# A transformer chain on one core: constants made early, the first layer's last closing on VectorE, weight loads moved

## The chip, the cores and the metric

The kernel runs on one core of one Trainium2 chip. The metric is the device time of that core in microseconds (us). The median of three runs of the kernel before is 1660.57 us (1658.11 to 1660.71). The work is in float32 throughout, so every matrix product on TensorE is issued as two passes, and counts in the trace are twice those in the code.

## The reference

Four layers follow one another on an activation `x` of 64 sequences of 64 tokens, each a row of 128 numbers; the same shape of context, `ctx`, goes beside it.

```python
x = L0(x, ctx)   # relative-position attention, 16 heads of 64 over ctx+x; LN, relu MLP, LN
x = L1(x, ctx)   # self attention and cross attention (16 heads of 8, masks), relu MLP; three LN
x = L2(x, ctx)   # a gate from pooled ctx, LN
x = L3(x, ctx)   # self and cross attention, then 8 experts, the best two of each token
# the end of L0:
out = layer_norm(x + ctx_heads @ Wo, ln1_g, ln1_b) * non_pad_mask
out = layer_norm(out + relu(out @ W1 + b1) @ W2 + b2, ln2_g, ln2_b) * non_pad_mask
```

A layer norm is `(x - mean) / sqrt(var + eps) * g + b` over the 128 numbers of a token.

## The kernel before

**Tiling.** The 4096 tokens are cut into 8 groups of 512. A group is a tile of 128 partitions by 512: four blocks of 128 tokens side by side.

**First layer** (`first_layer`, L381). One software pipeline, `for t in range(-REL, n)` (L627), runs over 64 steps: 8 groups times 8 pairs of heads. A step t issues parts of several pairs: the transposed weights and products of pair t, the scores of t+2, keys of t+3, the position scores of t+5. The emitted order is kept on every engine in this layer. Small jobs are hung onto single steps: `pads()` at 0, `later(t)` at 0 to 7, `block_diagonal()` from 12. After a group's eighth pair its closing generator `close` (L574) is started, and it is advanced once a step beside the next group: transpose, layer norm, affine, MLP, layer norm, affine. The last closing, of group 7, is not advanced there; it is handed on in `ends`, together with what is left of group 6.

**The norm.** `normalise` (L289) takes mean and variance on VectorE, then the inverse root: with `quick` false one power on GpSimd, with `quick` true eleven small operations on VectorE (`inverse_root`, L276). With a mask (`npm`) GpSimd multiplies the factor by it, and VectorE applies mean and factor in four operations. `affine` (L325) then multiplies by `g` and adds `b` times the mask, three operations on GpSimd; the product of `b` and mask is in a tile `oT`, of which there are two.

**Second part** (`other_layers`, L987). `drive` (L152) runs the generators of the remaining phases in rounds: self attention, cross attention and so on for each group, new ones admitted every few rounds, and the leftover closings `ends` in front of them. A further generator, `fill` (the experts), is stepped once a round. Here the framework's scheduler orders each engine's instructions by priorities; the order is fixed when the kernel is built, and each engine works strictly in it. PSUM tiles come from 7 rotating buffers (`pmm`, L120) and one further buffer, `extra` (L123), which holds the attention products `av` and some small results. All DMAs of the SyncE and ScalarE queues share eight completion semaphores in turn, so a new one waits for the eighth last one.

**Between the two parts.** The memory of the first layer is given up and taken anew, so the first instructions of the second part wait for the last of the first. In the kernel before these stand there:

- on ScalarE's queue, the loads of `w2l`, `in3`, `wo3` and `rw` (L992 to L995), and later the sixteen expert weight loads of `load_expert` (L1548), called in `layer2` (L1297);
- on GpSimd, the constants of the router and the experts (`desc`, `tri`, `ones`, `tok`, `base0`, `start`, `limit`, `index`, `lane`: memsets, `iota`s, one select), then memsets of two tiles `vb`;
- on VectorE, the copies of those `iota`s into float32;
- on TensorE, four transposes of the experts' biases into `extra` (`pfb`, L1520), which VectorE copies into `fc1bT` (L1523).

Of the kernel before, what the change touches and what calls it, by code (L numbers as in the profile page):

```python
# [9 lines left out]
I32 = mybir.dt.int32  # L10
# [3 lines left out]
ALU = mybir.AluOpType  # L14
AX = mybir.AxisListType

P = 128
B = 64
S = 64
D = 128  # L20
NB = 8
T = NB * S
NBLK = T // P
# [74 lines left out]
def kernel(ctx: ExitStack, tc: tile.TileContext, a: dict, out: bass.AP):  # L98
# [16 lines left out]
    def wtile(shape, tag, bufs, dtype=F32):  # L115
        if tag in COMMON:
            return pools["common"].tile(shape, dtype, tag=tag, bufs=COMMON[tag], name=tag)
        return pools["work"].tile(shape, dtype, tag=tag, bufs=bufs, name=tag)
# [22 lines left out]
    def v3(ap, n):  # L141
        return ap.rearrange("p (a b) -> p a b", a=n)
# [5 lines left out]
    def mid(ap, n):  # L148

        return ap.unsqueeze(1).to_broadcast([ap.shape[0], n, ap.shape[1]])  # L150
# [65 lines left out]
    yrows = dram.tile([2 * B * S, D], F32, tag="yrows", name="yrows", bufs=1)  # L216
    PADS = 5

    def block_diagonal():

        nc.vector.tensor_reduce(
            hm, ident.rearrange("p (h e) -> p h e", e=8), axis=AX.X, op=ALU.add
        )
        nc.vector.tensor_reduce(
            m4, hm.rearrange("p (g j) -> p j g", j=4), axis=AX.X, op=ALU.add
        )

        for i in range(2):  # L230
            yield
            blocks = wtile([P, 3, P], "T", 4)
            for k in range(3):
                nc.vector.tensor_tensor(
                    blocks[:, k, :].rearrange("p (h e) -> p h e", e=8),
                    mid(bd_small[:, 3 * i + k, :], 16),
                    last(hm[:, :], 8),
                    ALU.mult,
                )
            yield  # L240
            pt = pmm("bdt")
            for k in range(3):
                nc.tensor.transpose(pt[:, k * P : (k + 1) * P], blocks[:, k, :], ident)
            turned = wtile([P, 3, P], "T", 4)
            nc.vector.tensor_copy(turned, v3(pt[:, 0 : 3 * P], 3))
            yield
            pf = pmm("fold")
            nc.tensor.matmul(pf[:, 0:P], lhsT=turned[:, 2, :], rhs=turned[:, 1, :], start=True, stop=True)
            nc.tensor.matmul(pf[:, P : 2 * P], lhsT=turned[:, 0, :], rhs=wo1[:, i, :], start=True, stop=True)
            yield  # L250
            nc.vector.tensor_copy(qk1[:, i, :], pf[:, 0:P])
            nc.vector.tensor_copy(wo1[:, i, :], pf[:, P : 2 * P])
# [36 lines left out]
    def normalise(dst, src, npm=None, width=D, quick=False):  # L289

        st = wtile([P, NBLK, 6], "st6", 4)
        mv = wtile([P, NBLK, 2], "mv", 4)
        rs = wtile([P, NBLK], "rs", 4)
        for k in range(NBLK):
            nc.vector.bn_stats(st[:, k, :], src[:, k * P : (k + 1) * P])
        for k in range(NBLK):
            nc.vector.bn_aggr(mv[:, k, :], st[:, k, :])
        nc.vector.tensor_scalar(
            rs, mv[:, :, 1:2].rearrange("p a b -> p (a b)"), EPS, None, ALU.add
        )  # L300
        if quick:
            inverse_root(rs)
        else:
            nc.gpsimd.tensor_tensor(rs, rs, nhalf, ALU.pow)
        if npm is not None:
            nc.gpsimd.tensor_tensor(rs, rs, npm, ALU.mult)
        yield
        if npm is None:
            nm = wtile([P, NBLK], "nmr", 4)
            nc.vector.scalar_tensor_tensor(  # L310
                nm, mv[:, :, 0:1].rearrange("p a b -> p (a b)"), -1.0, rs, op0=ALU.mult, op1=ALU.mult
            )
        for k in range(NBLK):
            ks = slice(k * P, (k + 1) * P)
            if npm is None:
                nc.scalar.activation(
                    dst[:, k * width : k * width + D], src[:, ks], AF.Identity,
                    scale=rs[:, k : k + 1], bias=nm[:, k : k + 1],
                )
            else:  # L320
                nc.vector.tensor_scalar(
                    dst[:, ks], src[:, ks], mv[:, k, 0:1], rs[:, k : k + 1], ALU.subtract, ALU.mult
                )

    def affine(dst, src, g, b, npm=None):  # L325
        nc.gpsimd.tensor_tensor(v3(dst[:, :], NBLK), v3(src[:, :], NBLK), mid(row(g), NBLK), ALU.mult)
        if npm is None:
            nc.gpsimd.tensor_tensor(v3(dst[:, :], NBLK), v3(dst[:, :], NBLK), mid(row(b), NBLK), ALU.add)
        else:
            bn = wtile([P, T], "oT", 2)  # L330
            nc.gpsimd.tensor_tensor(
                v3(bn[:, :], NBLK), mid(row(b), NBLK), last(npm, D), ALU.mult
            )
            nc.gpsimd.tensor_tensor(dst, dst, bn, ALU.add)

    LANDED = mybir.DependencyInfo(mybir.DependencyClass.Sync, mybir.DependencyReason.DATA)

# [43 lines left out]
    def first_layer():  # L381
# [191 lines left out]

        def close(g, zT):  # L574
            npm = cols[:, _C["npm"][0] + NBLK * g : _C["npm"][0] + NBLK * (g + 1)]
            o1 = turned(zT, "z", 4)
            yield
            yield from normalise(o1, o1, npm)
            affine(o1, o1, "l0_g1", "l0_be1", npm)
            yield  # L580
            o1T = turned(o1)
            add_row(o1, "l0_b2")
            yield
            hs = []
            hidden(o1T, w1_0, "l0_b1", hs, range(2))
            yield
            hidden(o1T, w1_0, "l0_b1", hs, range(2, 4))
            yield
            pf = tokens_by(lambda c: hs[c], lambda c: w2_0[:, c, :], NFC)
            yield  # L590
            z = wtile([P, T], "z", 2)
            nc.vector.tensor_tensor(z, pf, o1, ALU.add)
            yield from normalise(z, z, npm)
            affine(xs[g], z, "l0_g2", "l0_be2", npm)

        pad = wtile([P, PADS, ROWW], "pad", 1)

# [29 lines left out]
        for t in range(-REL, n):  # L627
# [40 lines left out]
                pads()  # L668
            if 0 <= t < 8:
                later(t)  # L670
            if t == 12:
                folds = block_diagonal()
            if t >= 12:
# [313 lines left out]
    def other_layers(ends):  # L987
# [1 line left out]
        in3 = wtile([P, 2, 3 * D], "in3", 1)  # L989
        wo3 = wtile([P, 2, D], "wo3", 1)  # L990
        rw = wtile([P, NE], "rw", 1)
        nc.scalar.dma_start(w2l, a["w2l"])  # L992
        nc.scalar.dma_start(in3, a["in3"])
        nc.scalar.dma_start(wo3, a["wo3"])
        nc.scalar.dma_start(rw, a["rw"])  # L995

        bkm = wtile([P, 2, 4], "bkm", 1)
        for i, name in enumerate(("sa_in_b", "ca_in_b")):
            nc.vector.tensor_scalar(bkm[:, i, :], m4, col(name, 1), None, ALU.mult)

        desc = wtile([P, NE], "desc", 1)
        for e in range(NE):
            nc.gpsimd.memset(desc[:, e : e + 1], float(NE - e))
        tri = wtile([P, P], "tri", 1)
        make_upper_triangular(nc, tri[:, :], diag=False)
        ones = wtile([P, P], "ones", 1)
        nc.gpsimd.memset(ones, 1.0)

        toki = wtile([P, NG * NBLK], "toki", 1, I32)
        nc.gpsimd.iota(toki, pattern=[[P, NG * NBLK]], base=0, channel_multiplier=1)  # L1010
        tok = wtile([P, NG * NBLK], "tok", 1)
        nc.vector.tensor_copy(tok, toki)

        base0 = wtile([P, NE], "base0", 1)
        bases = {0: base0}
        basei = wtile([P, NE], "basei", 1, I32)
        nc.gpsimd.iota(basei, pattern=[[REGION * P, NE]], base=0, channel_multiplier=0)
        nc.vector.tensor_copy(base0, basei)


        vbs = [wtile([P, NB, 8, 18], f"vb{i}", 1) for i in range(2)]
# [404 lines left out]
        def router(g, hT, x, zx):  # L1426
# [67 lines left out]
            for n in range(2):  # L1494
# [6 lines left out]
                for k in range(NBLK):  # L1501
# [13 lines left out]
                            )  # L1515
                    done["scatters"][h].append(sc.ins)
            done["routed"] += 1

        fb = cols[:, _C["fc1_b"][0] : _C["fc1_b"][1]].rearrange("p (e c) -> p c e", c=NFC)
        pfb = extra("pfb")  # L1520
        for c in range(NFC):
            nc.tensor.transpose(pfb[0:NE, c * P : (c + 1) * P], fb[:, c, :], ident)
        nc.vector.tensor_copy(fc1bT, v3(pfb[0:NE, :], NFC))  # L1523

        drive(
            [(self1, "attention"), (cross1, "attention"), (forward1, "light"), (layer2, "light"),
             (self3, "attention"), (cross3, "attention")],
            {"attention": 4, "light": 2},
            ends,
            experts(),  # L1530
        )

    done = {"scatters": [[] for _ in range(NH)], "routed": 0, "exponentials": False}
# [13 lines left out]

    def load_expert(e):  # L1548
        es = slice(e * D, (e + 1) * D)
        nc.scalar.dma_start(fcw[:, 0:NFC, es], a["fc1"][e].rearrange("p (c k) -> p c k", k=P))  # L1550
        nc.scalar.dma_start(fcw[:, NFC:, es], a["fc2"][e].rearrange("(f c) d -> c f d", c=P))

    start = mtile([P, NE], "start")
    limit = mtile([P, REGION], "limit")
    index = mtile([P, max(NSLOT)], "index")
    lane = mtile([P, 1], "lane")
    for dst, step, n, mult in (
        (start, REGION * P, NE, 0), (limit, P, REGION, 0), (index, 1, max(NSLOT), 0), (lane, 0, 1, 1)
    ):
        it = mtile([P, n], f"iota{n}", I32)  # L1560
        nc.gpsimd.iota(it, pattern=[[step, n]], base=0, channel_multiplier=mult)
        nc.vector.tensor_copy(dst, it)
    endbase = [mtile([P, NE], f"endbase{h}") for h in range(NH)]
    fc1bT = mtile([NE, NFC, P], "fc1bT")
    with stage("att", psx=1):
# [73 lines left out]
```

## Time and profile before

| | |
|---|---|
| median of three runs | 1660.57 us |
| the profiled execution's own time | 1656.37 us |
| its span, first to last instruction | 1654.6 us |
| busy in the span: VectorE, ScalarE, GpSimd | 1166.5, 992.8, 888.3 us |
| mean granted TensorE clock | 0.951 |
| first layer, 0 to 713 us: TensorE busy | 695.11 us, clock 1.00 |
| passage, 713 to 790 us: TensorE busy | 61.77 of 77 us, clock 0.82 |

The table's first three rows are three things: runs without a profiler, the one execution that the trace shows, and the stretch of it between first and last instruction. In the listings a row has its start, its duration, the engine, the operation, what it writes and reads, how many instructions are merged, and in brackets how long the engine was idle before and what released it. A row merged from several instructions starts with the first and covers the whole of them. "PEld" is the loading of a weight tile into TensorE, "ACTq" and "SPq" the issuing of DMAs by ScalarE's and SyncE's sequencers. All instructions carry line 77, since a helper records them, so rows are told apart by their tiles. In tables by stretch each engine has its busy us and, in brackets, its instructions; then come the granted clock (1.00 is full), the share of the DMA engines and GB/s.

### The profile page before, as it was taken

To read this page: it belongs to the slowest core of one execution; us is meant where nothing else is said; L and a number is where in the kernel's file an instruction comes from. 1 tells how busy PE (TensorE), PEld (TensorE's weight loads), DVE (VectorE), ACT (ScalarE), POOL (GpSimd) and SP (SyncE) were. 2 spreads that over 40 slices of the span, in tenths; PEclk is the share of its full clock that TensorE was granted. 3 is DMA by queue.
4 is the path that set the end of the run, shared out by engine and by line. 5 is a ranking of instruction groups with operands and counts; after the bars stand their busy time and mean duration, and the time that the engine had idled before them with its cause. 6 is when DMAs were issued, how large, how long until landed. Compare 5 with 4: busy or idle time off the path is not lost.

```text
span 1654.6 us, 45059 instructions
## 1 busy us (share of the span) xinstructions
PE 1524.2 (92%) x17469; PEld 1132.4 (68%) x17469; DVE 1166.5 (70%) x3226; ACT 992.8 (60%) x2711; POOL 888.3 (54%) x852
## 2 busy tenths in 40 slices
PE   6999999999999999978888999989989899868995
PEld 4666666666666666646666676666767667668995
DVE  4767686867677677758897688676776688756555
ACT  4666455555655565535776565656777777427774
POOL 2546373645555564666887576644332223367543
PEclk9999999999999999979999899898999899759998
DMA  6776544545455554241001000000000000113244
GB/s 171 157 172 160 141 138 127 136 132 144 121 144 132 144 135 107 56 140 34 12 15 31 24 24 20 9 8 8 2 2 15 21 2 7 35 54 86 74 116 125
DMA packets 215540, 131.40 MB, mean 79 GB/s; under 512 B 38416, under 2 KB 201490, under 8 KB 215328
## 3 DMA queue, kind: packets, MB, share of 16 engines
q1 hardware_dynamic: 186016, 90.52, 22.9%
q10 hardware_dynamic: 24992, 29.54, 5.7%
q0 software_dynamic: 4320, 8.47, 1.5%
q8 instruction: 139, 2.28, 0.6%
q14 instruction: 73, 0.60, 0.1%
HBM read 66.48 MB, written 62.47 MB: 78 GB/s over the span
## 4 chain that ended last, share of the span: by engine, by line
PE 65%; DVE 18%; ACT 6%; POOL 6%; DMA 3%; issue 2%; SPq 0%; ACTq 0%; DVEq 0%; POOLq 0%
PE av L77 8%; PE psv L77 8%; PE proj L77 7%; PE psk L77 6%; PE f L77 6%; PE pt L77 6%; PE tok L77 5%; DVE mx L77 4%; PE pbd L77 4%; DVE s L77 4%; PE psc L77 4%; PE acc L77 3%; PE tr L77 2%; ACT z L77 2%; PE sc L77 2%
## 5 line engine op out<-in xcount | busy, mean ns | idle before, releaser
L77 ACT ACTIVATE s<-s,nm 128x128 f32<-128x128 f32 x512 | 198.1, 388 | 236.8 <-DVE nm L77 220.5
L77 POOL TENSOR_TENSOR s<-s,sm 128x512 f32<-128x512 f32 x128 | 130.4, 1040 | 208.7 <-DVE sm L77 208.7
L77 PE MATMUL pt<-ident,s 128*128 128x128 f32 x1536 | 213.0, 282 | 19.3 <-DVE s L77 12.1
L77 POOL TENSOR_TENSOR s<-s,mx 128x512 f32<-128x512 f32 x160 | 164.4, 1046 | 99.8 <-DVE mx L77 93.6
L77 PEld LDWEIGHTS pt<-ident,s 128*128 128x128 f32 x1536 | 177.0, 145 | 41.2 <-issue 17.7
L77 POOL TENSOR_TENSOR skew<-skew,mb 128x512 f32<-128x512 f32 x128 | 159.9, 1270 | 70.7 <-DMA skew<-scr 70.2
L77 ACT ACTIVATE pT<-pt 128x512 f32<-128x512 f32 x256 | 140.5, 600 | 79.6 <-PE pt L77 71.3
L77 POOL TENSOR_TENSOR rs<-rs,nhalf 128x4 f32<-128x4 f32 x72 | 73.3, 1018 | 151.9 <-DVE rs L77 144.1
L77 PEld LDWEIGHTS av<-vb,pT 128*64 128x64 f32 x4096 | 132.2, 143 | 23.4 <-issue 12.4
L77 PE MATMUL av<-vb,pT 128*64 128x18 f32 x4096 | 140.4, 215 | 6.8 <-DVE o L77 4.8
L77 DVE TENSOR_REDUCE mx<-s 128x8 f32<-128x512 f32 x160 | 102.8, 675 | 40.1 <-ACT s L77 40.1
L77 PE MATMUL psv<-wv,kv 128*128 128x256 f32 x512 | 127.4, 392 | 0.0
L77 PE MATMUL psk<-kv,wk 128*128 128x512 f32 x256 | 127.0, 618 | 0.0
L77 PE MATMUL sc<-km,qs 32*64 32x256 f32 x2048 | 106.3, 422 | 8.9 <-ACT qs L77 4.4
L77 DVE COPY pT<-pt 128x512 f32<-128x512 f32 x128 | 82.0, 681 | 36.9 <-PE pt L77 36.9
L77 PEld LDWEIGHTS psv<-wv,kv 128*128 128x128 f32 x512 | 92.2, 189 | 15.1 <-issue 1.0
L77 PEld LDWEIGHTS pbd<-rT,qp 64*128 64x128 f32 x1024 | 62.1, 187 | 58.3 <-DVE qp L77 56.5
L77 PEld LDWEIGHTS av<-pT,v 128*64 128x64 f32 x2048 | 66.8, 138 | 50.9 <-issue 31.3
L77 DVE TENSOR_TENSOR s<-sc,mb 128x512 f32<-128x512 f32 x128 | 82.4, 680 | 25.0 <-PE sc L77 25.0
L77 POOL DMA_INDIRECT yrows<-km,tob x71 | 71.2, 1004 | 53.1 <-DVE tob L77 26.4
L77 DVE TENSOR_TENSOR s<-psc,skew 128x512 f32<-128x512 f32 x128 | 87.4, 683 | 13.9 <-issue 6.3
L77 ACT ACTIVATION_READ_ACCUMULATOR s<-s,nm 128x1 f32 x512 | 95.6, 187 | 0.0
(256 smaller groups left out, 3523.3 us busy)
## 6 DMA issues: line engine op xcount, KB each, us to landing
scr<-stage SPq DMA_DIRECT2D x64, 516.0 KB, 4.8
skew<-scr SPq DMA_DIRECT2D x128, 256.0 KB, 4.3
hrows<-pad ACTq DMA_DIRECT2D x53, 325.0 KB, 2.5
ctx<-in_ctxT SPq DMA_DIRECT2D x24, 256.0 KB, 2.6
km<-hrows SPq DMA_DIRECT2D x71, 65.0 KB, 2.0
fcw<-in_fc ACTq DMA_DIRECT2D x16, 256.0 KB, 4.0
kv<-in_xT SPq DMA_DIRECT2D x8, 256.0 KB, 4.9
kv<-in_ctxT SPq DMA_DIRECT2D x8, 256.0 KB, 5.4
```

The costliest lines, as they stand in the source:

```text
L77: ins = it(*args, **kw)
```

## The change

1. The router's and experts' constants are made in step 11 of the first layer by a function `constants()`, in tiles that live through the kernel.
2. `normalise` and `affine` of the last closing (`g == NG - 1`) run on VectorE: inverse root, multiplication by the mask, `g` and `b`. The two products of `b` and mask stay on GpSimd, issued at the closing's start.
3. A generator `prepared` goes before the experts': after four rounds it issues the loads of `in3`, `wo3`, `rw` and `w2l` on ScalarE's queue, after four more the transposes and the copy to `fc1bT`.
4. The sixteen expert weight loads go to SyncE's queue.

```diff
+    def constants():
+        for e in range(NE):
+            nc.gpsimd.memset(desc[:, e : e + 1], float(NE - e))
+        make_upper_triangular(nc, tri[:, :], diag=False)
+        nc.gpsimd.memset(ones, 1.0)
+        nc.gpsimd.iota(toki, pattern=[[P, NG * NBLK]], base=0, channel_multiplier=1)
+        nc.vector.tensor_copy(tok, toki)
...
+            nc.gpsimd.iota(it, pattern=[[step, n]], base=0, channel_multiplier=mult)
+            nc.vector.tensor_copy(dst, it)
...
-            nc.gpsimd.tensor_tensor(rs, rs, npm, ALU.mult)
+            (nc.vector if quick else nc.gpsimd).tensor_tensor(rs, rs, npm, ALU.mult)
...
+    def shift_of(b, npm):
+        bn = wtile([P, T], "oT", 2)
+        nc.gpsimd.tensor_tensor(v3(bn[:, :], NBLK), mid(row(b), NBLK), last(npm, D), ALU.mult)
+        return bn
+
-    def affine(dst, src, g, b, npm=None):
+    def affine(dst, src, g, b, npm=None, shift=None):
+        if shift is not None:
+            nc.vector.tensor_tensor(v3(dst[:, :], NBLK), v3(src[:, :], NBLK), mid(row(g), NBLK), ALU.mult)
+            nc.vector.tensor_tensor(dst, dst, shift, ALU.add)
+            return
...
+            quick = g == NG - 1
+            shift = [shift_of(b, npm) if quick else None for b in ("l0_be1", "l0_be2")]
             o1 = turned(zT, "z", 4)
             yield
-            yield from normalise(o1, o1, npm)
-            affine(o1, o1, "l0_g1", "l0_be1", npm)
+            yield from normalise(o1, o1, npm, quick=quick)
+            affine(o1, o1, "l0_g1", "l0_be1", npm, shift[0])
...
-            yield from normalise(z, z, npm)
-            affine(xs[g], z, "l0_g2", "l0_be2", npm)
+            yield from normalise(z, z, npm, quick=quick)
+            affine(xs[g], z, "l0_g2", "l0_be2", npm, shift[1])
...
+            if t == 11:
+                constants()
             if t == 12:
                 folds = block_diagonal()
...
-        nc.scalar.dma_start(w2l, a["w2l"])
...
+        def prepared(gen):
+            for _ in range(4):
+                yield
+            nc.scalar.dma_start(w2l, a["w2l"])
+            nc.scalar.dma_start(in3, a["in3"])
+            nc.scalar.dma_start(wo3, a["wo3"])
+            nc.scalar.dma_start(rw, a["rw"])
+            for _ in range(4):
+                yield
+            fb = cols[:, _C["fc1_b"][0] : _C["fc1_b"][1]].rearrange("p (e c) -> p c e", c=NFC)
+            pfb = extra("pfb")
+            for c in range(NFC):
+                nc.tensor.transpose(pfb[0:NE, c * P : (c + 1) * P], fb[:, c, :], ident)
+            nc.vector.tensor_copy(fc1bT, v3(pfb[0:NE, :], NFC))
+            yield from gen
...
-            experts(),
+            prepared(experts()),
...
     def load_expert(e):
         es = slice(e * D, (e + 1) * D)
-        nc.scalar.dma_start(fcw[:, 0:NFC, es], a["fc1"][e].rearrange("p (c k) -> p c k", k=P))
-        nc.scalar.dma_start(fcw[:, NFC:, es], a["fc2"][e].rearrange("(f c) d -> c f d", c=P))
+        nc.sync.dma_start(fcw[:, 0:NFC, es], a["fc1"][e].rearrange("p (c k) -> p c k", k=P))
+        nc.sync.dma_start(fcw[:, NFC:, es], a["fc2"][e].rearrange("(f c) d -> c f d", c=P))
```

Built, the changed kernel differs from the one before in the engines' orders only at step 11 and, in the second part, in about the first hundred instructions of each engine; from there on the orders are the same.

More of the change, by code (lines that the diff above doesn't have):

```diff
@@ L217 @@
     PADS = 5
+    desc, tri, ones, tok, base0, start, limit, index, lane = (
+        ctile([P, n], name)
+        for name, n in (
+            ("desc", NE), ("tri", P), ("ones", P), ("tok", NG * NBLK), ("base0", NE),
+            ("start", NE), ("limit", REGION), ("index", max(NSLOT)), ("lane", 1),
+        )
+    )
+    def constants():
[3 more added lines that the diff above has]
+        nc.gpsimd.memset(ones, 1.0)
+        toki = wtile([P, NG * NBLK], "toki", 1, I32)
+        nc.gpsimd.iota(toki, pattern=[[P, NG * NBLK]], base=0, channel_multiplier=1)
+        nc.vector.tensor_copy(tok, toki)
+        basei = wtile([P, NE], "basei", 1, I32)
+        nc.gpsimd.iota(basei, pattern=[[REGION * P, NE]], base=0, channel_multiplier=0)
+        nc.vector.tensor_copy(base0, basei)
+        for dst, step, n, mult in (
+            (start, REGION * P, NE, 0), (limit, P, REGION, 0), (index, 1, max(NSLOT), 0), (lane, 0, 1, 1)
+        ):
+            it = wtile([P, n], f"iota{n}", 1, I32)
+            nc.gpsimd.iota(it, pattern=[[step, n]], base=0, channel_multiplier=mult)
+            nc.vector.tensor_copy(dst, it)
     def block_diagonal():
@@ L329, in affine @@
         else:
[L330 to L334, printed above, removed]
+            nc.gpsimd.tensor_tensor(dst, dst, shift_of(b, npm), ALU.add)
     LANDED = mybir.DependencyInfo(mybir.DependencyClass.Sync, mybir.DependencyReason.DATA)
@@ L991, in other_layers @@
         rw = wtile([P, NE], "rw", 1)
-        nc.scalar.dma_start(w2l, a["w2l"])
-        nc.scalar.dma_start(in3, a["in3"])
-        nc.scalar.dma_start(wo3, a["wo3"])
-        nc.scalar.dma_start(rw, a["rw"])
         bkm = wtile([P, 2, 4], "bkm", 1)
@@ L999, in other_layers @@
             nc.vector.tensor_scalar(bkm[:, i, :], m4, col(name, 1), None, ALU.mult)
[L1001 to L1014, printed above, removed]
         bases = {0: base0}
-        basei = wtile([P, NE], "basei", 1, I32)
-        nc.gpsimd.iota(basei, pattern=[[REGION * P, NE]], base=0, channel_multiplier=0)
-        nc.vector.tensor_copy(base0, basei)
         vbs = [wtile([P, NB, 8, 18], f"vb{i}", 1) for i in range(2)]
@@ L1517, in router @@
             done["routed"] += 1
[L1519 to L1523, printed above, removed]
+        def prepared(gen):
[13 more added lines that the diff above has]
+            yield from gen
         drive(
@@ L1549, in load_expert @@
         es = slice(e * D, (e + 1) * D)
-        nc.scalar.dma_start(fcw[:, 0:NFC, es], a["fc1"][e].rearrange("p (c k) -> p c k", k=P))
-        nc.scalar.dma_start(fcw[:, NFC:, es], a["fc2"][e].rearrange("(f c) d -> c f d", c=P))
[L1553 to L1562, printed above, removed]
+        nc.sync.dma_start(fcw[:, 0:NFC, es], a["fc1"][e].rearrange("p (c k) -> p c k", k=P))
+        nc.sync.dma_start(fcw[:, NFC:, es], a["fc2"][e].rearrange("(f c) d -> c f d", c=P))
     endbase = [mtile([P, NE], f"endbase{h}") for h in range(NH)]
```

## The prediction

> **What bounds the kernel now.** I read the table of stretches first, then the chain of waits, then the order in time of three places that the change touches. In the first layer TensorE is busy 695.11 of 713 us. Then comes a hole:
>
> ```profile
> 710.00:720.00 10.00, 5.86 (x24) 2.85 (x20) 8.17 (x36) 4.18 (x8) 6.65 (x26) 0.70 0.52 154
> 720.00:730.00 10.00, 3.34 (x37) 1.81 (x38) 7.76 (x23) 3.72 (x9) 8.30 (x9) 0.50 0.40 123
> 750.00:760.00 10.00, 7.42 (x113) 6.46 (x112) 9.93 (x19) 3.28 (x6) 8.88 (x10) 0.75 0.07 16
> ```
>
> Columns: stretch, TensorE, its weight loads, VectorE, ScalarE, GpSimd, clock. TensorE idles 10.8 us of 710 to 730 and has half its clock; from 750 it is VectorE that is full. The chain of waits between 780 and 860 us lies on VectorE too (mx 26.9% and s 22.1% of it), so what VectorE loses there stays. The hole from near (order in time):
>
> ```profile
> 715.75 3.21 POOL L77 MEMSET vb<- 128x1152 f32 x6
> 715.76 2.08 DVE L77 CAST tok<-toki 128x32 f32<-128x32 int32 x1 [0.37 <-POOL toki L77]
> 715.82 0.58 ACT L77 COPY z<-tr 128x512 f32<-128x512 f32 x1 [16.23 <-POOL basei L77]
> 719.04 1.26 POOL L77 TENSOR_TENSOR x<-z,rows 128x512 f32<-128x512 f32 x1
> 719.12 1.33 DVE L77 TENSOR_SCALAR mb<-mb 128x256 f32<-128x256 int32 x1 [0.26 <-DMA mb<-in_mask_tgt]
> 720.37 0.86 DVE L77 BATCH_NORM_STATS2 st<-z 128x6 f32<-128x128 f32 x4
> 722.74 1.02 POOL L77 TENSOR_TENSOR rs<-rs,nhalf 128x4 f32<-128x4 f32 x1
> 724.08 1.11 DVE L77 TENSOR_SCALAR z<-z,mv,rs 128x128 f32<-128x128 f32 x4 [2.20 <-POOL rs L77]
> 725.33 1.27 POOL L77 TENSOR_TENSOR z<-z,rows 128x512 f32<-128x512 f32 x1 [1.29 <-DVE z L77]
> 726.68 1.26 POOL L77 TENSOR_TENSOR z<-z,oT 128x512 f32<-128x512 f32 x1
> 728.00 1.12 PE L77 MATMUL tr<-ident,z 128*128 128x128 f32 x4 [5.76 <-POOL z L77]
> ```
>
> The copied z stands ready at 716.40, but its statistics start at 720.37, behind casts and masks on VectorE; then power, norm and affine pass between VectorE and GpSimd until TensorE transposes at 728.00. Mark the second and fifth row: a 128x32 cast takes 2.08 us and ends with GpSimd's big memsets; a mask takes 1.33, ending just after GpSimd's x (720.30). I went through all VectorE operations that read and write SBUF alone and start inside a 1.0 to 1.3 us GpSimd operation (mb, rs, nmr, ag, pool, z by mean, z<-z,x): over fifty, and all but one end with or after it; those that read PSUM do not care.
>
> **Step 11.** In the first layer:
>
> ```profile
> 156.11 2.04 POOL L77 TENSOR_TENSOR s<-s,sm 128x512 f32<-128x512 f32 x2
> 158.17 1.29 DVE L77 COPY pT<-pt 128x512 f32<-128x512 f32 x2 [0.34 <-PE pt L77]
> 161.44 1.15 PE L77 MATMUL av<-pT,v 128*64 128x64 f32 x32
> ```
>
> The constants go behind s<-s,sm on GpSimd: they took 0.55 + 0.31 + 0.20 + 0.27 + 0.29 + 0.15 + 0.13 at 714.3 to 715.8, some 1.45 us in a row. So they end near 159.6, and six casts on VectorE, which wait for them, near 159.8; behind these are queued the two copies pT, now to 161.1 instead of 159.46. TensorE wants pT at 161.44: nothing is lost, by 0.3 us. The next iteration has idle VectorE time (1.22 us before v, 1.10 before stage), ScalarE's exponentials start 1.5 us late and free a PSUM buffer of psk at about 166.4, which pbd wants at 166.22. I take +0.2; bounds 0 and +1.5 (the whole row lost). A gain is excluded: TensorE has no hole there.
>
> **First norm of the last closing.** Gone from the hole: 1.45 us of GpSimd, 0.47 us of TensorE (pfb), the casts. ScalarE's z copy no longer waits for the issues of in3, wo3, rw (0.51 to 0.53 each): it comes some 1.0 us earlier. The memsets move to 714.4 to 717.5 and block VectorE's z of group 6 to about 716.4. By the compiled order statistics now stand ahead of the masks: they start near 717.8, 2.6 us earlier. Then, without conflict: statistics and mean 1.15, mask 0.3, rs and eleven steps of the root at 0.2 each (the root at 1336.0 to 1337.4 shows this pace) 2.4, two masks 0.6, mask product 0.2, z four times 1.11, two products of 0.7 (z<-tok,x, same shape, 0.68): 7.2, so tr at 725.0, 3.0 us early.
>
> Here a rule weighs against the change. The Trainium skill, GPSIMD Engine Reference (4.1 Engine selection), sends elementwise work to VectorE, as GpSimd takes about twice as long for two inputs; the rows agree (1.27 against 0.68), which alone would give 1.2 us per affine. But SBUF — State Buffer (SBUF: two separate sides) says that GpSimd and a VectorE operation with two SBUF inputs, or in a two-port mode, take one port pair for a whole instruction, and the other blocks. By the rows above that holds here. In 717.6 to 722.9 GpSimd has x, x, oT, and x with the bias, back to back (1.27 + 1.27 + 1.05 + 1.27 and the gaps). The root's steps each depend on the last, so one or two pass between two GpSimd operations. About ten steps with masks are left at 722.9: 2.6 us; then 1.11 and 1.4, and tr at about 728.2. By the first rule -3.0, by the second +0.2. I take +0.2, since all its parts have rows.
>
> **Products behind it.** tr to tok is TensorE's own work, 16.4 us in both. But in the compiled order ScalarE now has qs (0.59) and the issue of ff1 (0.35) ahead of h, which before began at 740.05:
>
> ```profile
> 740.05 0.68 ACT L77 ACTIVATE h<-proj,cols 128x512 f32<-128x512 f32 x1
> 740.94 3.39 PE L77 MATMUL tok<-w,h 128*128 128x128 f32 x28
> 746.60 1.02 POOL L77 TENSOR_TENSOR rs<-rs,nhalf 128x4 f32<-128x4 f32 x1 [5.01 <-DVE rs L77]
> 747.94 1.11 DVE L77 TENSOR_SCALAR z<-z,mv,rs 128x128 f32<-128x128 f32 x4 [1.42 <-POOL rs L77]
> 754.59 3.31 PE L77 MATMUL av<-vb,pT 128*64 128x18 f32 x64 [2.58 <-DVE o L77]
> ```
>
> h then ends some 0.95 us later and tok, whose second matmul needs it, follows: +0.8 (0 to +1.0; a gain is excluded, as tok starts when TensorE is free).
>
> **Second norm of the last closing, and pfb.** Before, from VectorE's z<-tok,z at 744.44: statistics to 746.52, 1.42 of waiting for GpSimd, z 1.11, eight s and mx 4.8, rec and o to 754.53, eight more to 759.2, rec, o to 760.0, mb to 761.05, then 3.83 us of waiting for TensorE's sc, and s at 764.87. After, in the compiled order, on one engine: statistics 2.1; five root steps 1.0; eight s and mx 4.8; two steps, rec, o 0.95; four steps and the mask product 1.0; eight s and mx with z 1.11 and two products of 0.68 among them 7.3; the fc1bT copy (8x512 from PSUM, priced at 0.69 like pT; its own 1.92 was blocked by a memset) 0.7; mb 0.3; rec, o 0.75. That is 18.9 us. The port: GpSimd subtracts mx from s in eight operations of 1.04 there, and these meet two root steps (0.5 and 0.8), the second product (0.45) and mb (0.85): +2.6, bounds 0 and +7 (each of eight meets one). Sum 21.5, so s at 744.44 + 21.5 = 765.9, against 764.87: +1.0. The 3.83 us of waiting are what hides 5.4 us of added VectorE work less the 1.42 no longer waited for.
>
> Does that cover hold? pfb takes `extra` after o, and the next av in `extra` waits for the fc1bT copy, a new wait: behind av in TensorE's queue stand five score products and the transposes of o. TensorE reaches it after pfb 0.7, pt 2.0, proj 1.9, tr 0.6, pt 1.1, sc 0.8 from o (754.6), at 761.7; the copy ends at about 764.0. So TensorE waits 2.3 us there, and each further us on VectorE is paid in full. Bounds of this part: -1.6 (no conflict) and +5.5 (all meet). I take +0.8, since TensorE finds the transposes of o free a little earlier in the groups that follow: the eight av matmuls (0.65) stand behind sc there.
>
> **DMA edits, at nothing.** The sixteen issues took 0.39 to 0.63 on ScalarE, one with a wait of 3.87 before h; but h began at 733.60 and its proj ended at 733.57, and the 4.42 before pT at 746.62 lay beside VectorE's norm. If those covers go, they are worth up to 1 us each, in which case tr must be earlier. On SyncE's queue they stand behind three mb and three ctx, already issued, and ahead of the next mb, which before was issued at 738.90 when its buffer came free. Sixteen loads of 256 KB at 210 to 260 GB/s, the rows of 720 to 740, take some 16 to 20 us from 718: done by 738, so mb is not late, by little; late, it would cost VectorE's mb at 741 what it overruns, up to 2 us. in3, wo3, rw behind the vb copies on ScalarE have 5 us of idle time before T.
>
> **Sum.** +0.2, +0.2, +0.8, +0.8: +2.0 us on the profiled execution: span 1654.6 to 1656.6, its own time 1656.37 to 1658.4. It was 4.2 us under the runs' median, so I add the difference to the median: 1660.57 + 2.0 = 1662.6.
>
> **Rivals.** *The port does not matter (faster).* If the root's steps slip between GpSimd's operations, tr comes 3.0 us early, tok still loses 0.8, and the second part takes -1.6 (18.9 us of VectorE from the start of z<-tok,z, against TensorE's av at about the same point): 0.2 - 3.0 + 0.8 - 1.6 = -3.6, so 1657.0; with the hole shorter the clock may also recover sooner (proj x4 took 3.78 at half clock, 1.9 at full), up to -1.9 more. For it: the masks and root steps are short, and a rule can be kinder to 128x4 tiles. Against: rs of 128x4 took 0.58 to 1.06 in all five cases inside a GpSimd operation.
>
> *VectorE becomes the bound in the second norm (slower).* The place is 750 to 765; the mechanism is that fc1bT's copy, at the end of a queue that now carries norm and affine, holds `extra`, and with it TensorE's av, sc and the next s. It decides as soon as that copy ends behind TensorE's arrival at 761.7, which I already expect; with all eight subtractions in the way it is +5.5, with the +0.8 and +0.4 ahead +6.7: 1667.3; with half of them +4, 1664.6. For it: VectorE is 9.93 of 10 busy there and stays the chain to 860. Against: several steps have s or mx, from PSUM or reductions, between them.
>
> *Step 11 alone costs.* If pT slips past 161.44 by the margin of 0.3, TensorE, at 5.00 of 5.00 there, loses up to 1.5: 1664.
>
> That the edits do not take place is excluded by the compiled orders.
>
> **Chances.** The likeliest, the sum as it stands (within 0.2%, that is 3.3 us, about what a measurement of this kernel can tell from no change): 0.45, own range 1660 to 1664. Port free: 0.23, 1655 to 1658. VectorE bound: 0.25, 1664 to 1668. Step 11: 0.07. The last two count as slower for all that exceeds 1663.9: 0.31 together. Faster (under 1657.3) 0.22, within 0.47. The range 1656.5 to 1666.5 leaves one in ten out at each end.
>
> **What would show it.** In the profile after: casts of tok to lane near 159.8 and av still near 161.4; statistics of the last closing near 718 and its root steps of 0.2 broken by ones of about 1.2 that end with GpSimd's x and oT; tr of z within 1 us of 728.4; tok x28 about 1 us later against tr; fc1bT's copy the releaser of an av, and s of the third group near 767. If tr is near 725, the port step is wrong; if av is released by TensorE itself and s comes before 765, the second norm's sum is; if TensorE has a hole near 161, step 11's.

## The result, and the profile after

| | before | after |
|---|---|---|
| median in one series (5 runs each) | 1660.53 us | 1668.48 us |
| ratio | | 1.0043, interval 1.0025 to 1.0061 |
| the profiled execution's own time | 1656.37 us | 1669.58 us |
| its span | 1654.6 us | 1667.8 us |
| mean granted TensorE clock | 0.951 | 0.944 |

The changed kernel is slower by some 7 us (4 to 10), above the predicted 1662.6 and above the range, which ended at 1666.5. In two of the four later series every kernel, that of before too, took some 30 us longer, all of it behind 1400 us and so behind what is read here; each ratio below is to the runs of before in its own series.

To see where the time goes, I took the start of every TensorE and VectorE instruction in the profile after, subtracted that of the same instruction in the profile of before, and took the median around some times of before:

```
time in before (us)   60    180    690    743    790    960   1250   1400   1640
after               +4.0   +3.8   +3.8   +2.5   +9.3   +7.9  +12.2  +12.3  +13.2
```

Three steps of this lag stand out (between 790 and 960 us 1.4 come back, and behind 1400 one more is lost). The first 4 us come before 60 us, ahead of step 11, where both kernels are the same: from 30 to 40 us TensorE's clock was 0.66, in before 1.00. From 690 to 743 the new kernel gains 1.3, and from 743 to 790 it loses 6.8, 5.5 together. The third, +4.3 between 1015 and 1250, is taken up below. So I look at 743 to 790 first. The table of stretches of the profile after (columns as in the prediction; times here stand 2.5 to 3.8 us later than in before):

```profile
724.00:734.00 10.00, 2.98 (x22) 1.53 (x7) 9.60 (x28) 2.27 (x5) 4.33 (x5) 0.50 1.03 299
754.00:764.00 10.00, 6.64 (x46) 4.49 (x46) 9.86 (x24) 5.13 (x9) 4.42 (x4) 0.83 0.00 0
```

The hole behind the first layer is there as before, at half clock. VectorE is as full from 754 as it was from 750; what has changed is TensorE: 46 instructions in that stretch, against 113 in 750 to 760 of before, and 79 there in 751.5 to 761.5, the same stretch less the lag of 2.5 us. The order in time of the same profile says why:

```profile
743.40 3.39 PE L77 MATMUL tok<-w,h 128*128 128x128 f32 x28
756.77 0.83 PE L77 MATMUL pfb<-ident,cols 128*8 128x128 f32 x4 [2.98 <-DVE o L77]
764.76 0.67 DVE L77 COPY fc1bT<-pfb 8x512 f32<-8x512 f32 x1
765.48 2.17 PE L77 MATMUL av<-vb,pT 128*64 128x18 f32 x64 [1.30 <-DVE fc1bT L77]
768.87 1.29 DVE L77 TENSOR_TENSOR s<-sc,mb 128x512 f32<-128x512 f32 x2 [0.33 <-PE sc L77]
```

At the place where before had av (754.59) now stands pfb, which takes `extra`. (Its four transposes are four instructions in the trace; products count twice there, transposes once.) Its copy to fc1bT is ready to run by 757.6 but lies at the end of VectorE's queue, until 764.76; only then may av write into `extra`, 8.4 us behind its old place when the lag of 2.5 is taken off. TensorE waits 1.30 us for it. What follows is seen if the table of stretches is cut to 3.42 us, the step in which the clock changes here. For TensorE alone (stretch, busy and instructions, clock, DMA share, GB/s):

```profile
763.88:767.30 3.42, 2.12 (x64) 0.99 0.17 38
767.30:770.72 3.42, 3.42 (x48) 0.50 0.02 5
770.72:774.14 3.42, 3.42 (x37) 0.50 0.00 0
774.14:777.56 3.42, 3.42 (x27) 0.50 0.00 0
777.56:780.98 3.42, 3.42 (x40) 0.51 0.02 5
780.98:784.40 3.42, 3.42 (x77) 1.00 0.00 0
```

Behind the stretch with the wait, TensorE has no idle time for 13.7 us, and spends all of it at half clock: the pt of eight matmuls takes 1.91 us instead of 1.04. The queue of products that av held up is worked off at half speed, and more av and a tok follow before the next full set of scores:

```profile
769.27 2.96 PE L77 MATMUL av<-vb,pT 128*64 128x18 f32 x50
772.16 2.08 PE L77 MATMUL tok<-wo,oT 128*128 128x128 f32 x8
775.87 1.04 PE L77 MATMUL av<-vb,pT 128*64 128x18 f32 x14
778.75 2.01 PE L77 MATMUL sc<-km,qs 32*64 32x256 f32 x32
```

In before only two stretches at this place are at half clock (columns as in the table of 3.42 us):

```profile
754.86:758.28 3.42, 3.42 (x64) 0.52 0.00 0
758.28:761.70 3.42, 3.42 (x12) 0.50 0.17 38
```

### The profile page after: what moved, and what is told of

It reads as the page before. It is cut to its first block, busy times and chain, and to the rows that moved or that the text cites. A ratio compares the mean times of both kernels' runs of the same rounds, so it can differ in the third digit from the quotient of the medians.

```text
span 1667.8 us, 45077 instructions
## 1 busy us (share of the span) xinstructions
PE 1536.9 (92%) x17469; PEld 1142.6 (69%) x17469; DVE 1178.0 (71%) x3254; ACT 993.4 (60%) x2711; POOL 882.2 (53%) x844
## 4 chain that ended last, share of the span: by engine, by line
PE 62%; DVE 18%; POOL 6%; ACT 6%; issue 4%; DMA 3%; ACTq 0%; POOLq 0%; SPq 0%; DVEq 0%
PE av L77 8%; PE psv L77 8%; PE proj L77 7%; PE psk L77 7%; PE pt L77 6%; PE pbd L77 4%; PE tok L77 4%; DVE mx L77 4%; PE psc L77 4%; DVE s L77 4%; PE acc L77 3%; PE f L77 3%; PE sc L77 2%; PE tr L77 2%; ACT z L77 2%
## 5 line engine op out<-in xcount | busy, mean ns | idle before, releaser
L77 PE MATMUL pt<-ident,s 128*128 128x128 f32 x1536 | 216.8, 286 | 18.2 <-DVE s L77 11.2
L77 PEld LDWEIGHTS pt<-ident,s 128*128 128x128 f32 x1536 | 180.4, 147 | 39.8 <-issue 17.7
```

What stands on the lines that cost most here:

```text
L77: ins = it(*args, **kw)
```

## The experiments

Theory A: the copy to fc1bT, late on VectorE, holds `extra`; TensorE waits and then works at half clock. Theory B: the 5 us of norm and affine added to VectorE are the loss, whatever stands in `extra`. Theory C: the stretches at half clock fall where they will, and the profile of after met a bad draw. A fourth reading is that av's being late is itself the loss, and the clock only goes along. The losses from 743 to 790 us below are read from one profile of each run.

**e1_again**, the changed kernel once more.

> The changed kernel again, unedited, to learn what of the 13.2 us between the two profiled spans repeats. Theory A (second norm: the copy of fc1bT holds the PSUM buffer extra, TensorE idles at 763 to 765, falls to half clock and works off its products late): the stretch from 740 to 790 us loses 6 to 7 us in this profile too. Theory C (the clock's windows fell unluckily in that one execution): half-clock windows lie elsewhere, the stretch loses under 3 us here. The 3.8 us lost before 45 us, where no instruction was changed, are expected gone or still there by chance; if they are there again, they belong to the change. Time 1664 to 1669.

Ratio 1.0012 (0.9988 to 1.0037): the time alone decides nothing here. Its profile does: from 743 to 790 it loses 6.7 us, with four stretches at half clock in a row after the wait. The draw of theory C came out the same twice.

**e2_pfb_back**, transposes and copy back in front of the rounds; norms stay on VectorE.

```diff
+        fb = cols[...]; pfb = extra("pfb"); # transposes and copy to fc1bT, moved here
         def prepared(gen):
...
-            # the same five lines
```

> The changed kernel with the transposes of the experts' biases and the copy to fc1bT put back ahead of the second part's rounds; all else as changed. Theory A (the copy of fc1bT holds extra, and TensorE's av waits behind it): the wait of av for fc1bT is gone, the stretch 740 to 790 loses under 2 us, time about 5 us less than the changed kernel's, near 1662. Theory B (VectorE's own 5 us of norm and affine are the loss): under 1.5 us better, 1666 to 1668. Theory C (unlucky clock windows): anything from 1661 to 1669 with no order among the edits.

Ratio 0.9986 (0.9965 to 1.0007), which overlaps that of e1; 743 to 790: +0.1 us. The copy no longer stands in the passage's queue, and the loss is gone with VectorE as loaded as in after.

**e3_norm2_back**, second norm and affine on GpSimd again, pfb in the rounds.

```diff
-            shift = [shift_of(b, npm) if quick else None for b in ("l0_be1", "l0_be2")]
+            shift = [shift_of(b, npm) if quick else None for b in ("l0_be1",)]
...
-            yield from normalise(z, z, npm, quick=quick)
-            affine(xs[g], z, "l0_g2", "l0_be2", npm, shift[1])
+            yield from normalise(z, z, npm)
+            affine(xs[g], z, "l0_g2", "l0_be2", npm)
```

> The changed kernel with the second norm and affine of the last closing on GpSimd again, the first one still on VectorE. Theory A: fc1bT's copy comes some 4 us earlier, but av still waits for it; half of the 6 us comes back, 1664 to 1666. Theory B (VectorE's added work in the second norm): nearly all of it comes back, 1661 to 1663. Theory C: no order.

Ratio 0.9995 (0.9974 to 1.0016); +0.2 us. pfb stands at 755.59, as in after, but its copy comes 4.6 us behind it, not 8.0, and av doesn't wait for it:

```profile
760.21 0.67 DVE L77 COPY fc1bT<-pfb 8x512 f32<-8x512 f32 x1
761.88 2.05 PE L77 MATMUL av<-vb,pT 128*64 128x18 f32 x64
```

Nearly all of the loss is gone, as theory B had forecast here, and A not (it had half): the wait doesn't shrink with the queue, it is gone as soon as the copy is there before TensorE. So it takes both: pfb in the rounds, and a VectorE queue that is some 3.4 us longer. The lateness of av alone is not the loss: here av comes 6.3 us behind its old place (lag of 1.0 taken off; 8.4 in after), and it costs nothing.

**e4_norms_back**, both norms on GpSimd, pfb in the rounds (`quick` and `shift` taken out).

> The changed kernel with both norms of the last closing on GpSimd, so only constants, loads and pfb are moved. If the port makes the first norm on VectorE no gain, as the prediction had it, this is within 1 us of the kernel with the second norm alone put back. If the first norm gained (the trace after shows 1.3 us gained over the first hole), it is 1 to 2 us slower than that kernel.

Ratio 0.9984 (0.9964 to 1.0004); +0.2 us, with av 6.3 us late as in e3. From 690 to 743 it gains 2.0 us, e3 only 1.4; more on this at e11.

**e5_pfb_psm**, the changed kernel with pfb in one of the seven rotating buffers.

```diff
-            pfb = extra("pfb")
+            pfb = pmm("pfb")
```

> The changed kernel with one word changed: the tile of the experts' biases is one of the seven rotating PSUM buffers, no longer extra. Norms, copy to fc1bT and its place late in VectorE's queue stay. Theory A (av waits for extra, which the late copy holds): av comes before fc1bT, no four half-clock windows at 765 to 781, the stretch from 743 to 790 us loses under 1.5 us against the kernel before (the changed kernel lost 6.8 and 6.7). Theory B (VectorE's 5 us more of work there are the loss by themselves): it still loses 5 to 7 us.

Ratio 0.9995 (0.9979 to 1.0010); 743 to 790: 0.0 us. This is the one that parts A and B, since all of the norms' work is still on VectorE. (No run of the changed kernel stands in this series; what is compared with it is the loss in the passage.) Its order in time:

```profile
754.10 2.46 PE L77 MATMUL av<-vb,pT 128*64 128x18 f32 x64 [2.54 <-DVE o L77]
762.07 0.67 DVE L77 COPY fc1bT<-pfb 8x512 f32<-8x512 f32 x1
```

The copy is as late in VectorE's queue as in after (764.76 there, with 2.5 us of lag), but nobody waits: av has gone 8 us ahead of it, where it stood in before. And the clock, in stretches of 3.42 us again, for TensorE of the same kernel:

```profile
762.30:765.72 3.42, 2.44 (x58) 1.00 0.12 28
765.72:769.14 3.42, 3.42 (x25) 0.51 0.00 0
769.14:772.56 3.42, 3.42 (x70) 1.00 0.02 5
```

One stretch at half clock behind a partly idle one, then full. Theory B is out.

**e6_copy_act**, the changed kernel with the copy on ScalarE.

```diff
-            nc.vector.tensor_copy(fc1bT, v3(pfb[0:NE, :], NFC))
+            nc.scalar.copy(fc1bT, v3(pfb[0:NE, :], NFC))
```

> The changed kernel with the copy to fc1bT made by ScalarE, which is idle there, in place of VectorE; extra as in the change. Theory A: extra comes free some 6 us earlier, the stretch from 743 to 790 us loses under 1.5 us. Theory B: it still loses 5 us or more, as the norm stays on VectorE.

Ratio 1.0001 (0.9983 to 1.0020); +0.6 us. ScalarE stood idle for it, and lets `extra` go some seven us earlier (lags taken off):

```profile
753.74 0.60 PE L77 MATMUL pfb<-ident,cols 128*8 128x128 f32 x4 [2.98 <-DVE o L77]
754.38 0.57 ACT L77 COPY fc1bT<-pfb 8x512 f32<-8x512 f32 x1 [3.00 <-PE pfb L77]
755.01 3.56 PE L77 MATMUL av<-vb,pT 128*64 128x18 f32 x64
```

**e7_consts_only**, the kernel before with `constants()` in step 11 and nothing else.

> The kernel before with nothing but the constants made in step 11. The prediction took +0.2 us (0 to 1.5) for step 11: lag from 140 to 180 us 0 to 1.5. At the passage 1 to 2 us are gained, as GpSimd's 1.45 us and VectorE's casts are gone from it, if theory A is right that the passage's gains come from what left it and not from the norms; under 0.5 if they come from the norms or loads.

Ratio 1.0003 (0.9987 to 1.0019); step 11 (140 to 180 us) -0.3, 690 to 743 -0.3, 743 to 790 +0.2 us. Nothing is won or lost by it.

**e8_consts_loads**, constants and moved loads, norms and pfb as before.

> The changed kernel with both norms on GpSimd and the experts' bias transposes put back: constants at step 11 and the weight loads moved, nothing else. Beside the kernel with constants alone it tells what the loads do: the prediction took 0. If they gain, 1 to 2 us more at the passage. Time 0.1 to 0.2% under the kernel before, the best of the set, if the edits' parts add up.

Ratio 1.0004 (0.9989 to 1.0019); 690 to 743 -1.7, 743 to 790 +0.1 us. Against e7 the moved loads gain 1.4 us in the passage, which the total doesn't show: the 0.1 to 0.2% that were expected did not come.

**e9_before_again**, the kernel before once more, and **e10_after_third**, the changed kernel a third time, side by side with it.

> The kernel before, unedited, against itself: what a profile of the same code moves by. If the lags outside the passage (up to 4 us before 60 us, up to 4 us either way from 890 to 1250) come from where the clock's windows fall, this profile has such lags too, of 1 to 5 us, with half-clock windows at other places, and at the passage (690 to 790) under 1 us. If they belong to the change, it follows the first profile of before within 1 us everywhere. Ratio 1.000.

> The changed kernel a third time, on the chip and in the rounds of the kernel before against itself. Theory A: again 6 to 7 us lost from 743 to 790 with three or four half-clock windows from about 766, and ratio 1.002 to 1.005, interval clear of 1.

e9: ratio 1.0012 (0.9997 to 1.0027), and its profile follows the first at -0.9 to -1.4 us all the way from 60 to 1400 us; 743 to 790: +0.1. So the lags of 1 to 5 us outside the passage, which it should have shown if they come from the clock alone, are not in it. e10: 1.0044 (1.0020 to 1.0068), and +7.8 us, with five stretches at half clock. So the loss is the change's, and repeats: 6.8, 6.7, 7.8. In e10, before 60 us the same code is 2.7 us later than in the first profile of before, so part of the first 4 us of after is not even steady from run to run.

**e11_norm1_back**, only the first norm and affine on GpSimd again.

```diff
-            shift = [shift_of(b, npm) if quick else None for b in ("l0_be1", "l0_be2")]
+            shift = [shift_of(b, npm) if quick else None for b in ("l0_be2",)]
...
-            yield from normalise(o1, o1, npm, quick=quick)
-            affine(o1, o1, "l0_g1", "l0_be1", npm, shift[0])
+            yield from normalise(o1, o1, npm)
+            affine(o1, o1, "l0_g1", "l0_be1", npm)
...
-            affine(xs[g], z, "l0_g2", "l0_be2", npm, shift[1])
+            affine(xs[g], z, "l0_g2", "l0_be2", npm, shift[0])
```

> The changed kernel with the first norm and affine of the last closing on GpSimd, the second still on VectorE and fc1bT's copy still late in its queue. Theory A: the loss from 743 to 790 stays, 5 to 7 us. The first norm's own worth: if the shared port takes its gain away, as predicted, the lag at 743 is within 1 us of the changed kernel's; if VectorE gained 3 us there, it is 3 us later.

Ratio 1.0030 (1.0011 to 1.0050); 690 to 743 -1.9, 743 to 790 +6.8 us. The loss stays, with the same wait of 1.30 us of av for fc1bT (at 760.68) and the same four stretches. The first norm has no part in it. It is no cheaper on VectorE: with the loads moved, 690 to 743 gains 1.7 to 2.0 us where that norm is on GpSimd (e4, e8, e11) and 0.3 to 1.6 where it is on VectorE (eight profiles; the same code gave 1.3, 0.9 and 0.4 in after, e1 and e10, so the size is not known better).

**e12_pfb_three_times**, the changed kernel with the four transposes issued three times over, to fill TensorE's wait; the engines' orders are otherwise the same, but for the places of two ScalarE masks.

```diff
-            for c in range(NFC):
-                nc.tensor.transpose(...)
+            for _ in range(3):
+                for c in range(NFC):
+                    nc.tensor.transpose(...)
```

> The changed kernel with the four bias transposes issued three times over (twelve in place of four, into the same buffer; the result is the same), in front of the same work in the same order. It gives TensorE 1.0 to 1.7 us more to do ahead of the products that wait for the fc1bT copy, and nothing else. Theory A with the clock: the 1.3 us of waiting are filled, the stretch of 3.4 us that held them is full or nearly so, and the four stretches at half clock behind it (13.7 us) do not come or are fewer; the loss between 743 and 790 falls from 6.8 to between 1 and 4 us although there is more work, and the time comes nearer to that of before (ratio 1.000 to 1.003). Rival A2, that the late attention products themselves (11 us behind their old place) cost the time and the clock only goes along: the loss stays at 6.8 or grows to 8.5 us, ratio 1.004 to 1.006. If the free-running position of the clock's stretches decides, either can come out; then the rows of the stretches tell: half clock behind a full stretch speaks against the wait as its cause.

Ratio 1.0035 (1.0012 to 1.0058); 743 to 790: +5.0 us. The wait was not filled: TensorE's later scores delay VectorE's s and with it the copy, and av waits 1.30 us again. On that point the expectation was wrong, and the run is no test of a filled wait; its loss lies between the 1 to 4 us expected with a filled wait and the 6.8 to 8.5 expected if av's lateness were the cost. But the clock's steps fell elsewhere:

```profile
762.07:765.48 3.41, 2.11 (x62) 1.00 0.17 38
765.48:768.89 3.41, 3.41 (x50) 0.51 0.02 5
...
772.31:775.72 3.41, 3.41 (x26) 0.50 0.00 0
775.72:779.13 3.41, 3.41 (x70) 0.99 0.02 5
```

Three stretches at half clock, one fewer than in after, and the loss 1.8 us smaller, with more to do. That gives a sum that can be tried on all profiles. A stretch at half clock costs half of 3.42, 1.71 us; I counted the stretches at half clock from 750 to 782 us, and set the loss against it:

| profile | half-clock stretches | loss 743 to 790, us |
|---|---|---|
| before, e2, e5, e6, e7, e8, e9 | 2 | 0.0 to +0.6 |
| e3, e4 | 1 | +0.2 |
| e12 | 4 | +5.0 |
| after, e1, e11 | 5 | +6.7 to +6.8 |
| e10 | 6 | +7.8 |

For after: 3 more than before, 5.1 us, and 1.7 are left; for e12 2 more, 3.4, 1.6 left; for e10 4 more, 6.8, 1.0 left. The remainder is near the wait for the copy (1.30 us). So of 6.8 us some five are the clock's and some one and a half are the wait's. e3 and e4, with one stretch fewer than before, gain nothing by it, so the sum holds for the loss and not for every passage.

How long the half clock lasts goes with what TensorE works on. In all fourteen profiles together, 45 stretches at half clock between 737 and 795 us had TensorE busy for 3 us or more. I took from each the time spent in av, whose matmuls move 18 columns (from the start of one matmul to that of the next). In 24 stretches av took less than 0.9 us, and the next stretch was at full clock each time. In 21 av took 0.97 us or more, and 20 were followed by another at half clock; the exception is in e5, from 755.5. In after av takes 1.73, 1.50 and 0.97 us of the first three stretches behind the wait, and nothing of the fourth, whose scores come just before the clock opens. No run changes av alone, so this is a rule of these profiles, and not shown as the cause.

## Why the prediction was wrong, step by step

**Step 11: right.** The profile after, around the constants:

```profile
160.07 2.04 POOL L77 TENSOR_TENSOR s<-s,sm 128x512 f32<-128x512 f32 x2
...
163.71 1.28 DVE L77 COPY pT<-pt 128x512 f32<-128x512 f32 x2
165.22 1.15 PE L77 MATMUL av<-pT,v 128*64 128x64 f32 x32
```

pT starts 5.5 us later than in before (158.17), 1.6 of them beyond the lag of 3.9; av 3.8 later (161.44), that is, not at all. From 140 to 180 us the lag changes by -0.1, predicted +0.2. In e1 and e2 it changed by +1.6 and +1.0, with the same step 11 as in the others (-0.4 to +0.2); I did not find why.

**First norm: the port, right; its surroundings a little too dear.** The order in time of the profile after:

```profile
722.74 1.27 POOL L77 TENSOR_TENSOR x<-x,oT 128x512 f32<-128x512 f32 x1
722.93 1.12 DVE L77 TENSOR_SCALAR root<-rs 128x4 int32<-128x4 int32 x1
724.10 1.05 POOL L77 TENSOR_TENSOR oT<-rows,cols 128x512 f32<-128x512 f32 x1
724.28 0.88 DVE L77 SCALAR_TENSOR_TENSOR rootb<-root 128x4 f32<-128x4 f32 x1
725.11 1.38 POOL L77 TENSOR_TENSOR x<-x,rows 128x512 f32<-128x512 f32 x1
725.29 1.22 DVE L77 TENSOR_TENSOR rootb<-rootb,rs 128x4 f32<-128x4 f32 x1
...
730.91 1.09 PE L77 MATMUL tr<-ident,z 128*128 128x128 f32 x4 [6.35 <-DVE z L77]
```

A root step on four numbers a partition takes 0.16 us when nothing is beside it; these three end with the GpSimd operation that runs next to them. (The prediction's count of such cases, all but one, is too clean: GpSimd's power of 128x4, rs<-rs,nhalf, held none of the six nmr and rs of 128x4 that start inside it between 1005 and 1117 us of before, which took 0.10 to 0.16 us. None of these lies in this passage.) tr comes 2.9 us later than in before, where the first layer had left a lag of 3.8: 0.9 early, predicted 0.2 late. The rival without the port (3.0 early) is refuted; the difference of a microsecond is about what the moved loads gained (e8 against e7, 1.4), which the prediction had put at nothing, with "up to 1 us each" if their cover went.

**Products behind it: +0.8 was predicted, and nothing was paid.** tok's 28 matmuls start 2.46 later than in before, less than tr (2.9). h started 2.6 later (742.66 against 740.05), so qs ahead of it did not make it late against tr, and it ended at 743.36, as TensorE came out of pt and four sc.

**Second norm, and pfb: here it failed.** The step said that TensorE reaches av at 761.7, that the copy ends at about 764.0, that s comes at 765.9, and took +0.8 for the whole. With the 2.5 us of lag at tok taken off, TensorE arrived at 761.7 (765.48 less the wait of 1.30), the copy ended at 762.9, and s came at 766.4. The queue was mapped well, and even the port was cheaper than feared. The step that failed is the price of the new wait for the copy: the prediction had the wait itself, and longer (2.3 us, measured 1.30), but +0.8 counts only the delay of s, with the groups behind it even catching up a little; measured are +6.8. What it left out is the clock: the wait falls into one of the clock's stretches, and the products queued behind it, av above all, are done at half clock for 13.7 us. That makes three stretches more than in before, by the sum above some 5.1 us of the 6.8. The prediction had used the clock only in the hole near 720, as a gain if the hole got shorter; it had to ask the same of the new wait.

**Rivals.** "VectorE becomes the bound in the second norm" is what happened, at its place (750 to 765) and by its mechanism (the copy at the end of the queue, holding `extra`). Its price, up to +6.7 us, was right by accident: it came from conflicts at the port, and these stayed small. And VectorE's load alone isn't the bound: e5 and e6 carry it without loss. "Step 11 alone" is refuted by e7.

**What stays open.** The third step of the profile after, +4.3 from 1015 to 1250 us: mean clock there is 0.91 in after, e10 and e11, 0.93 in before and e9, 0.94 in e6 and e8, though the engines' orders are the same. e2, e4, e5 and e7 lose 3.0 to 4.3 there with no loss in the passage or in the time, and e12, with the loss in the passage, only 0.7, so it doesn't mark the change; that a shift of some microseconds decides on which side of a wait the clock's steps fall is a guess. Why stretches full of av are followed by more at half clock is open too. A kernel that puts other products between the late av and the next would test whether the order behind the wait, and not the wait, sets the loss; e12 did not fill the wait, and no run changed that order.

No version beats both kernels: the ratios of e2 to e8 all have 1 in their intervals. Norms on VectorE, constants and loads each buy about nothing in the time, and the loss comes from where one small result was put and which queue empties it.

## What to carry to other kernels

A small job moved to a "free" moment takes its buffer with it: ask which queue its last reader stands in, how far back, and who needs the buffer next; another buffer or an idle engine for the copy (one line each here) took the whole loss away. When a change adds a wait to the busiest engine, price not only the wait but the work queued behind it at the clock that it will then have; look which products are in that queue. And when two profiles differ by 13 us, line them up instruction by instruction first: only 5.5 of them could be put down to the change.

## What the runs showed of the hardware

- In after TensorE stayed at half clock for 13.7 us with 3.42 of 3.42 us busy in each of four stretches; in e10 for five stretches, the first with 2.79 us busy. The Trainium skill, TensorE: Matmul & The Clock Gate (What's actually happening), has the gate open again after one busy stretch of about 3.4 us, and close after an idle one. The step of 3.4 us agrees. But here a stretch with 2.12 us busy was enough to close it, and one to five passed until it opened. By the page's rule a wait of 1.30 us would not have closed it, and one stretch would have opened it: an estimate of 1.7 us at most for the clock, where the count of stretches gives some 5.
- Stretches with much the same busy time went both ways: with 2.1 us busy, 1.8 of them in av, the clock fell (after, from 763.8); with 2.1 us busy and no av it stayed full (e5, from 776.0).
- VectorE operations on 128x4 are held up by a 128x512 operation of GpSimd as larger ones are: 0.88 to 1.22 us instead of 0.16. SBUF — State Buffer (SBUF: two separate sides) states the lock, and these rows agree. GpSimd's power on 128x4 held none of six (0.10 to 0.16 us).
